# Attention in runs of four steps: four steps of logits, then their four products with v, instead of two and two

## Chip, cores, metric

One core of one Trainium2 chip. The metric is the device time of one execution in microseconds (us), median of several.

## The reference

A convolution block on x of shape (8, 512, 32, 32), fp32: group norm, a 1x1 convolution, then two bottlenecks, then a 1x1 convolution over everything and a residual. Each bottleneck is a 3x3 convolution, an attention over the 1024 positions with 4 heads of 64 channels, and a 1x1 convolution. What matters is the attention:

```python
q, k, v = (qkv[:, 0], qkv[:, 1], qkv[:, 2])
r = (rw + rh).reshape(1, HEADS, HD, hw)
logits = jnp.einsum('bhdi,bhdj->bhij', q, k + r) * HD ** (-0.5)
a = jax.nn.softmax(logits, axis=-1)
out = jnp.einsum('bhij,bhdj->bhdi', a, v)
```

8 images and 2 bottlenecks make 16 attention blocks. The kernel leaves the subtraction of the maximum out (and checks the sums at the end; a slower general path exists that is not taken here).

## The kernel before

A block has 4 groups: two pairs of heads (c) times two halves of 512 query positions. A group has 8 steps, each 128 key positions j. A step is: logits of both heads into one PSUM tile, exponential to SBUF (ScalarE), addition to acc for the softmax sums (VectorE), and the product with v, accumulated in PSUM. Steps go in pairs; a pair shares one pt tile. Each fp32 matmul here leaves two records in the trace (2048 records for the 1024 matmuls of the logits), so a step with its two heads has four records of logits and four of products. The code below is shortened; comments and `...` mark what was added and left out.

```python
def logits(pair):
    g, j0 = pair[0]
    c, half = groups[g]
    pt = act.tile([P, PAIR, 2, HALF], F32, tag="pt", name="pt", bufs=n_pt)     # n_pt = 3
    pts[pair[0]] = pt
    for i, (_, j) in enumerate(pair):
        ps = ps_big.tile([P, 2, HALF], F32, tag="big", name="l_ps")            # 3 buffers
        for hd in range(2):
            r = slice(hd * HD, (hd + 1) * HD)
            nc.tensor.matmul(ps[:, hd, :], kr[r, c, ts(j, P)], q[r, c, ts(half, HALF)],
                             start=True, stop=True)                            # L389
        nc.scalar.activation(pt[:, i], ps, AF.Exp, scale=SCALE)                # L393
    if j0 == 0:
        accs[g] = act.tile([P, 2, HALF], F32, tag="acc", name="acc", bufs=2)
        nc.vector.tensor_tensor(accs[g], pt[:, 0], pt[:, 1], ALU.add)          # L396
    else:
        for i in range(PAIR):
            nc.vector.tensor_tensor(accs[g], accs[g], pt[:, i], ALU.add)       # L399

def times_v(pair):
    ...
    for i, (_, j) in enumerate(pair):
        for hd in range(2):
            o = c * P + hd * HD
            nc.tensor.matmul(avs[g][hd * HD : (hd + 1) * HD, :], vT[:, j, o : o + HD],
                             pt[:, i, hd, :], start=(j == 0), stop=(j == NJ - 1))  # L410
    if j0 + PAIR == NJ:
        nc.scalar.copy(ao[:, c, ts(half, HALF)], avs.pop(g))

def divide(g):
    ...
    for hd in range(2):                                                        # L422
        nc.tensor.matmul(ps[hd * HD : (hd + 1) * HD, :], ones, acc[:, hd, :], start=True, stop=True)
    nc.vector.tensor_scalar(rs, ps, 1.0, None, ALU.mult, ALU.max, accum_out=smax[:, i : i + 1])
    nc.vector.tensor_reduce(smin[:, i : i + 1], rs, AX.X, ALU.min)
    nc.vector.reciprocal(rs, rs)                                               # L431
    nc.vector.tensor_tensor(dst, dst, rs, ALU.mult)                            # L433, dst in ao

for i in range(len(pairs) + 1):
    if i < len(pairs):
        logits(pairs[i])
    if i > 0:
        times_v(pairs[i - 1])
        g, j0 = pairs[i - 1][0]
        if j0 == 0 and g > 0:
            divide(g - 1)
divide(len(groups) - 1)
```

After the block comes the 1x1 convolution over ao (L555), first its half of the positions that does not need the last group, then the other half. As compiled, 12 of its 16 records stand ahead of the four that need the last group; these four are what the prediction calls the second half of L555.

## Time and profile before

| | before |
|---|---|
| time, median | 2860.6 us (2858.6 to 2861.4) |
| TensorE busy | 93% of the span |
| VectorE busy | 55% |
| ScalarE busy | 32% |
| a block, first logits to the first matmul on ao | 64.95 us, in 15 of 16 blocks |

The last line is taken from the starts of the matmuls in the trace. The lines of the page, the timeline and the waits are in the prediction.

### The profile page before, as it was taken

The page shows a single profiled execution, that of the slowest core. Times are in us where ns is not written, and L with a number is a line of the kernel's source. Part 1 is how long each engine was busy: PE and PEld are TensorE (multiplying, and loading weights), DVE is VectorE, ACT ScalarE, POOL GpSimd, SP SyncE. Part 2 cuts the span into 40 slices and gives each one's busy share as a digit, 9 for nine tenths or more (in the row PEclk, how much of TensorE's full clock was granted, in tenths as well). Part 3 has the DMA queues.
Part 4 walks back from the last instruction along what each step waited for, and adds up shares of the span by engine and source line. Part 5 has one row for each costly group of instructions (what it writes and reads, how often), then busy time and mean ns, then how long its engine had stood idle before and what let it go on. Part 6 is the DMA issues. An engine that isn't in the chain of part 4 may idle for free.

```text
span 2857.4 us, 24013 instructions
## 1 busy us (share of the span) xinstructions
PE 2670.4 (93%) x9506; PEld 1308.0 (46%) x9506; DVE 1582.2 (55%) x2116; ACT 923.6 (32%) x1209; POOL 72.0 (3%) x180
## 2 busy tenths in 40 slices
PE   2999999899998999989999899998999989999897
PEld 1626346263463534544354544545346363463633
DVE  5374734847347564575545665466644657437472
ACT  2242422424223332333324242242422424224241
POOL 2000000000000000000000000000000000000000
PEclk9999999999999999999999999999999999999998
DMA  9201011010110101101011000101012010110000
GB/s 356 87 1 67 1 59 67 1 67 2 57 67 1 67 15 44 67 16 51 30 42 55 34 34 30 63 34 61 6 44 81 1 67 1 52 67 1 0 1 31
DMA packets 25047, 130.23 MB, mean 46 GB/s; under 512 B 4448, under 2 KB 4960, under 8 KB 15200
## 3 DMA queue, kind: packets, MB, share of 16 engines
q1 hardware_dynamic: 14400, 97.00, 9.5%
q0 software_dynamic: 6784, 26.25, 2.4%
q10 hardware_dynamic: 3744, 5.37, 0.5%
q8 instruction: 77, 1.26, 0.2%
q14 instruction: 42, 0.34, 0.0%
HBM read 102.40 MB, written 26.21 MB: 45 GB/s over the span
## 4 chain that ended last, share of the span: by engine, by line
issue 56%; PE 37%; DVE 3%; POOL 1%; DMA 1%; ACT 0%; POOLq 0%; DVEq 0%; ACTq 0%; SPq 0%
PE ps L229 12%; PE l_ps L389 7%; PE av_ps L410 6%; PE c_mid L530 6%; PE c_end L530 3%; PE v_ps L360 2%; DVE acc L399 1%; DVE rs L431 1%; POOL out_dram L591 1%; PE s_ps L422 0%; DMA raw<-in_m_cv_w_dram 0%; DMA bnp<-in_cv_bn_dram 0%; DMA u<-u_new 0%; ACT pt L393 0%; POOL gr L320 0%
## 5 line engine op out<-in xcount | busy, mean ns | idle before, releaser
L393 ACT ACTIVATE pt<-l_ps 128x1024 f32<-128x1024 f32 x512 | 494.6, 1022 | 386.9 <-PE l_ps L389 386.9
L399 DVE TENSOR_TENSOR acc<-acc,pt 128x1024 f32<-128x1024 f32 x384 | 467.0, 1216 | 131.9 <-ACT pt L393 109.9
L389 PE MATMUL l_ps<-q,kr 64*128 64x512 f32 x2048 | 504.4, 613 | 0.0
L410 PE MATMUL av_ps<-pt,vT 128*64 128x512 f32 x2048 | 492.4, 604 | 0.0
L530 PE MATMUL c_mid<-v_in,u 128*128 128x256 f32 x1536 | 354.2, 388 | 70.7 <-DVE v_in L265 66.6
L530 PEld LDWEIGHTS c_mid<-v_in,u 128*128 128x128 f32 x1536 | 297.8, 195 | 127.1 <-issue 83.7
L389 PEld LDWEIGHTS l_ps<-q,kr 64*128 64x128 f32 x2048 | 177.6, 186 | 322.0 <-issue 314.5
L229 PE MATMUL ps<-xn,cv_sb 128*128 128x512 f32 x512 | 236.2, 624 | 48.1 <-DVE xn L325 48.1
L410 PEld LDWEIGHTS av_ps<-pt,vT 128*64 128x64 f32 x2048 | 125.6, 136 | 337.3 <-issue 264.2
L214 ACT ACTIVATE h<-ps,bh,sh 128x512 f32<-128x512 f32 x128 | 92.5, 773 | 521.5 <-PE ps L229 521.5
L229 PE MATMUL ps<-z,qkv_sb 128*128 128x512 f32 x512 | 229.2, 595 | 0.0
L229 PE MATMUL ps<-ypad,cv_sb 128*128 128x512 f32 x512 | 224.9, 592 | 0.0
L431 DVE RECIPROCAL rs<-rs 128x512 f32<-128x512 f32 x64 | 214.6, 3353 | 2.2
L530 PE MATMUL c_end<-v_in,u 128*128 128x256 f32 x768 | 181.9, 389 | 0.0
L229 PEld LDWEIGHTS ps<-xn,cv_sb 128*128 128x128 f32 x512 | 100.0, 198 | 178.3 <-issue 119.4
L530 PEld LDWEIGHTS c_end<-v_in,u 128*128 128x128 f32 x768 | 149.9, 195 | 22.6
L229 PEld LDWEIGHTS ps<-ypad,cv_sb 128*128 128x128 f32 x512 | 97.3, 190 | 122.5 <-issue 122.5
L279 DVE TENSOR_TENSOR sd<-c_mid,m 128x512 f32<-128x512 f32 x32 | 22.1, 691 | 228.3 <-ACT m L277 228.3
L229 PEld LDWEIGHTS ps<-z,qkv_sb 128*128 128x128 f32 x512 | 95.9, 190 | 106.5 <-issue 95.7
L396 DVE TENSOR_TENSOR acc<-pt 128x1024 f32<-128x1024 f32 x64 | 78.4, 1225 | 108.5 <-ACT pt L393 108.5
L585 DVE SCALAR_TENSOR_TENSOR t<-t,h 128x512 f32<-128x512 f32 x64 | 41.3, 687 | 171.2 <-ACT t L215 171.2
L277 ACT COPY m<-c_mid 128x512 f32<-128x512 f32 x32 | 18.7, 585 | 347.8 <-PE c_mid L530 347.8
(101 smaller groups left out, 2036.7 us busy)
## 6 DMA issues: line engine op xcount, KB each, us to landing
u<-u SPq DMA_DIRECT2D x64, 1152.0 KB, 6.9
x<-in_x_dram SPq DMA_DIRECT2D x32, 512.0 KB, 4.2
out_dram<-t POOLq DMA_DIRECT2D x64, 256.0 KB, 3.9
u<-u_new POOLq DMA_DIRECT2D x8, 1152.0 KB, 7.9
raw<-in_m_cv_w_dram SPq DMA_DIRECT2D x4, 1152.0 KB, 7.6
cv_sb<-in_cv_w_dram ACTq DMA_DIRECT2D x1, 2048.0 KB, 13.5
qkv_sb<-in_m_qkv_w_dram ACTq DMA_DIRECT2D x2, 768.0 KB, 12.9
cv_sb<-in_cv_w_dram ACTq DMA_DIRECT2D x1, 1024.0 KB, 9.1
```

The source lines that it names most:

```text
L214: nc.scalar.activation(h, ps, AF.Identity, scale=sh[:, k : k + 1], bias=bh[:, k : k + 1])
L229: nc.tensor.matmul(ps[:, half, :], w_of(k), rhs_of(k, half), start=(k == 0), stop=(k == nk - 1))
L360: nc.tensor.matmul(ps[:, j, :], z[:, k, ts(j0 + j, P)], qkv_sb[:, n, k, 2 * C : 3 * C], start=(k == 0), stop=(k == NM - 1),)
L389: nc.tensor.matmul(ps[:, hd, :], kr[r, c, ts(j, P)], q[r, c, ts(half, HALF)], start=True, stop=True,)
L393: nc.scalar.activation(pt[:, i], ps, AF.Exp, scale=SCALE)
L396: nc.vector.tensor_tensor(accs[g], pt[:, 0], pt[:, 1], ALU.add)
L399: nc.vector.tensor_tensor(accs[g], accs[g], pt[:, i], ALU.add)
L410: nc.tensor.matmul(avs[g][hd * HD : (hd + 1) * HD, :], vT[:, j, o : o + HD], pt[:, i, hd, :], start=(j == 0), stop=(j == NJ - 1),)
L431: nc.vector.reciprocal(rs, rs)
L530: nc.tensor.matmul(dst, us[k][:, pos, dx, :], vs[k][:, pos, :, dx : dx + F], start=(i == 0), stop=(i == NM * 3 - 1),)
L585: nc.vector.scalar_tensor_tensor(t, t, 1.0, h, ALU.add, ALU.mult)
L591: nc.gpsimd.dma_start(dst, t)
```

## The change

The intent is to alternate less often between logits and products. The change has a second side: before, the products of a pair stand one pair behind, after the logits of the next pair; now a run's products follow directly on its own logits. Nothing else is touched.

```diff
-            for i in range(len(pairs) + 1):
-                if i < len(pairs):
-                    logits(pairs[i])
-                if i > 0:
-                    times_v(pairs[i - 1])
-                    g, j0 = pairs[i - 1][0]
+            RUN = 2
+            for i in range(0, len(pairs), RUN):
+                for pair in pairs[i : i + RUN]:
+                    logits(pair)
+                for pair in pairs[i : i + RUN]:
+                    times_v(pair)
+                    g, j0 = pair[0]
                     if j0 == 0 and g > 0:
                         divide(g - 1)
             divide(len(groups) - 1)
```

## The prediction

> **What bounds the kernel now.** I read the page first, then the groups, then one attention block in the timeline, then the waits.
>
> ```profile
> PE 2670.4 (93%) x9506; PEld 1308.0 (46%) x9506; DVE 1582.2 (55%) x2116; ACT 923.6 (32%) x1209; POOL 72.0 (3%) x180
> ...
> L389 PE MATMUL l_ps<-q,kr 64*128 64x512 f32 x2048 | 504.4, 613 | 0.0
> L410 PE MATMUL av_ps<-pt,vT 128*64 128x512 f32 x2048 | 492.4, 604 | 0.0
> ```
>
> TensorE is busy 93% of the span, and the two attention groups (logits, L389; products with v, L410) show no idle time before them. So inside attention nothing but TensorE sets the pace, and a gain must come from TensorE itself. There are 16 attention blocks (8 images, 2 blocks each), each of 32 steps in 4 groups of 8. The profile's idle column cannot show the cost at stake, because a matmul's recorded time covers the pause ahead of the next one. The starts in the timeline can:
>
> ```profile
> 139.40 3.70 PE L389 MATMUL l_ps<-q,kr 64*128 64x512 f32 x16
> 143.03 1.94 PE L410 MATMUL av_ps<-pt,vT 128*64 128x512 f32 x8
> 144.90 0.70 PE L389 MATMUL l_ps<-q,kr 64*128 64x512 f32 x2
> ...
> 148.68 1.99 PE L389 MATMUL l_ps<-q,kr 64*128 64x512 f32 x8
> 150.60 1.94 PE L410 MATMUL av_ps<-pt,vT 128*64 128x512 f32 x8
> 152.47 0.70 PE L389 MATMUL l_ps<-q,kr 64*128 64x512 f32 x2
> ```
>
> Columns are start, extent, engine and group. A run of 8 logits records (two steps) lasts 150.60 - 148.68 = 1.92 us from start to next start; a run of 16, which the kernel before has once at the head of every block, lasts 143.03 - 139.40 = 3.63 us, not 3.84. So 8 more records cost 1.71 us, 0.428 us for each pair of records, and 0.21 us of each run of logits is fixed. For products, 8 records last 152.47 - 150.60 = 1.87 us; less 4 x 0.428 that leaves 0.15 us fixed. One round of logits and products is 152.47 - 148.68 = 3.79 us, with 0.353 us (unrounded starts) in its two changes of shape.
>
> **What bounds the end of a block.**
>
> ```profile
> 198.60 3.65 PE L410 MATMUL av_ps<-pt,vT 128*64 128x512 f32 x16
> 203.34 1.08 PE L422 MATMUL s_ps<-acc,ones 128*64 128x512 f32 x4 [1.09 <-DVE acc L399]
> 204.35 5.42 PE L555 MATMUL m_ps<-ao,m_sb 128*128 128x512 f32 x12
> 210.12 1.12 PE L555 MATMUL m_ps<-ao,m_sb 128*128 128x512 f32 x2 [0.36 <-DVE ao L433]
> ```
>
> There TensorE waits 1.09 us for VectorE's last addition to acc before it can form the last sums. The list of waits over the whole run (total, times, longest) says that this happens once in each block:
>
> ```profile
> PE s_ps L422 <- DVE acc L399: 17.7, 16, 1.4
> ```
>
> VectorE is late because, in each group, it has the division of the group before between its additions:
>
> ```profile
> 161.02 0.69 DVE L427 TENSOR_SCALAR_CACHE_REDUCE rs<-s_ps 128x512 f32<-128x512 f32 x1
> 161.63 0.08 DVE L427 DVE_READ_ACCUMULATOR rs<-s_ps 128x1 f32 x1
> 161.75 0.69 DVE L430 TENSOR_REDUCE smin<-rs 128x1 f32<-128x512 f32 x1
> 162.47 3.35 DVE L431 RECIPROCAL rs<-rs 128x512 f32<-128x512 f32 x1
> 165.74 1.16 DVE L399 TENSOR_TENSOR acc<-acc,pt 128x1024 f32<-128x1024 f32 x1
> 166.82 0.68 DVE L433 TENSOR_TENSOR ao<-ao,rs 128x512 f32<-128x512 f32 x1
> 167.42 3.88 DVE L399 TENSOR_TENSOR acc<-acc,pt 128x1024 f32<-128x1024 f32 x3
> ```
>
> From the start of rs to the end of the group's last addition is 171.30 - 161.02 = 10.28 us without a gap. That chain sets the end of a block, in both kernels.
>
> **What the Trainium skill says.** "TensorEngine Tiling (Array Packing)", section Tiling Modes, Key Properties: changing the tiling mode drains TensorE. Logits use 64 rows of the array (64*128 in the lines), products 64 columns (128*64), so each change of line is such a change, and the trace agrees: about 0.35 us per two changes. "TensorE: Matmul & The Clock Gate", Part 2, says that the engine pulls weight loads ahead of matmuls in flight. The trace agrees within a run, where the loads of L389 start a pair ahead (139.93 and 140.36 us, matmuls 0.43 us later), and shows it lost at a change, where the weight load sits idle 0.76 to 0.81 us and starts with its own matmul. "Trainium Kernel Development and Optimization", Reading a trace, warns that matmul busy time is a bad metric because matmuls are pipelined; here too, busy time is no measure of what is saved.
>
> **The change, part by part.** The compiled orders of VectorE, GpSimd and the load queue are the same instruction by instruction. On TensorE only the order of logits, products and the sums' matmuls moves; on ScalarE only the four copies of av_ps, which now stand ahead of the next group's exponentials. No instruction is added or removed.
>
> *Removed.* Before, a block runs 15 logits runs (the first double) and 15 product runs (the last double); after, 8 and 8. Seven rounds of two changes go: 7 x 0.353 = 2.47 us a block, 16 x 2.47 = 39.5 us in all, if nothing else sets the end.
>
> *Added waits inside a run of four steps.* PSUM holds three logits tiles, so step 4 waits for the exponential of step 1. In the existing run of 16 that starts at 140.57 and takes 1.02 us, so it is done 2.19 us into the run; the weight load of step 4 starts at 2.25 us, the normal 0.43 us after the one before. It fits by about 0.05 us: no wait. Step 4's exponential ends 4.94 us into the run (140.57 + 3.77), and its product comes at about 6.3 us. With the new copy of av_ps first at a group's head, the exponential still starts 1.18 us in (156.25, copy, 157.43), as elsewhere. The three pt buffers: each new pair needs the pair three back, already multiplied and added. No wait.
>
> *VectorE in the new order.* A round of four steps is 16 x 0.429 + 0.353 = 7.22 us; a group is two rounds and the sums' matmuls (0.86 us): 15.3 us, from 16.0 (172.25 - 156.25). VectorE has 8 steps in 7 additions and the division, from its first addition at 3.15 us after the group's start to the fourth step at about 7.0, when it takes rs (the sums are there at 6.5), and 10.28 us later, at 17.3 us, it is through: 2.0 us into the next group, whose first addition can only start at 3.15. So VectorE has about 1.1 us to spare per group: it does not set the pace, but it is filled to some 93%.
>
> *The end of a block.* The last group's products end 2 x 7.217 + 0.858 = 15.3 us after its start (the sums of the group before lie inside it), but acc is ready at 17.3. TensorE waits about 2.0 us for VectorE there, against 1.09 now. Measured from the start of the last group's first logits, acc is ready at 203.29 - 184.47 = 18.82 us before and 17.28 after: 1.54 us earlier. That start itself is 45.07 us into the block before and 6 x 7.217 + 2 x 0.858 = 45.02 after: 0.05 us. Sum: 1.59 us a block, 25.4 us over 16. What follows a block (second half of L555, activation, next convolution) hangs on it in series and moves with it. 2860.8 - 25.4 = 2835.4 us, 0.9% less.
>
> **The rivals.**
> 1. *VectorE does not set the end:* the full 39.5 us, 2821 us. For it: VectorE is busy only 55% in the page. Against it: the 1.09 us wait is already there in all 16 blocks.
> 2. *The fourth step waits for PSUM.* The margin is 0.05 us; if exponentials came 0.15 us late in each of 16 x 7 new runs, that takes back up to 17 us of TensorE time; part of this is hidden in the wait at the end: 2840 to 2850 us. Against it: 16 runs in this trace show the same tight fit with no stall.
> 3. *VectorE becomes the bound of every group,* for instance when its first addition comes later than 3.15 us or additions slow: then groups stretch towards 16 us and the gain dwindles: 2850 us or above. Against it: 1.1 us to spare.
> 4. *Products lose their lead over the exponentials,* since no logits stand between step 4 and its product: margin 1.3 us, so I give this little.
>
> **Range and chances.** The centre is the VectorE-bound sum. Down, towards rival 1, it can go as far as 2821 but hardly further; up, rivals 2 and 3 together. So 2824 to 2845. Over 2% faster would need 57 us, more than all removed changes are worth; over 2% slower needs 3.6 us more per block, for which no wait is in sight. Hence 0.02, 0.96, 0.02.
>
> **What would show it.** Right: in the timeline runs of 16 logits of 3.63 us and 16 products of about 3.58 us, 8 each per block; no idle before L389 and L410; the wait of s_ps for acc grown from 1.1 to about 2.0 us in 16 places; a block from first logits to its last sums' matmul of 62.3 us instead of 63.9. Wrong: idle before l_ps put down to pt (rival 2), idle of VectorE gone between groups (rival 3), idle before av_ps (rival 4), or an unchanged 1.1 us wait with 2821 us (rival 1). My sum fails if the cost of a change of shape is not the same in the longer runs of products, which the trace before shows only once a block.

## The result, and the profile after

The changed kernel takes 2836.6 us median (2831.5 to 2837.2, 4 runs). The ratio of the fast runs is 0.9913, 95% interval 0.9896 to 0.9930; it is the mean time of one kernel's fast runs over that of the other's of the same rounds, so not quite the ratio of the medians. The interval lies clear of 1: 24 us less. 25.4 had been predicted.

The first block in the timeline of TensorE (start, extent, engine, group):

```profile
139.67 3.70 PE L389 MATMUL l_ps<-q,kr 64*128 64x512 f32 x16
143.30 3.65 PE L410 MATMUL av_ps<-pt,vT 128*64 128x512 f32 x16
146.88 3.70 PE L389 MATMUL l_ps<-q,kr 64*128 64x512 f32 x16
150.52 3.65 PE L410 MATMUL av_ps<-pt,vT 128*64 128x512 f32 x16
```

Runs of 16 records, as forecast: logits 143.30 - 139.67 = 3.63 us, products 146.88 - 143.30 = 3.58 us, a round 7.21 us where two rounds took 7.57. No line shows idle time: the fourth step of logits does not wait for its PSUM tile, nor a product for its exponential.

The end of that block, in the timeline of TensorE:

```profile
196.40 3.65 PE L410 MATMUL av_ps<-pt,vT 128*64 128x512 f32 x16
201.97 1.08 PE L422 MATMUL s_ps<-acc,ones 128*64 128x512 f32 x4 [1.91 <-DVE acc L399]
202.97 5.42 PE L556 MATMUL m_ps<-ao,m_sb 128*128 128x512 f32 x12
```

and the list of waits over the whole run (total, times, longest):

```profile
PE s_ps L422 <- DVE acc L399: 30.9, 16, 2.3
```

The products are done 2.46 us earlier in the block than before (start of the sums less the wait, 60.39 us against 62.85 after the first logits), but the wait for acc has grown from 1.09 to 1.91 us: a third of the saving goes into a longer wait. From first logits to the last sums' matmul it is 201.97 - 139.67 = 62.30 us, from 63.94. The last group on VectorE, in its timeline:

```profile
187.84 1.23 DVE L396 TENSOR_TENSOR acc<-pt 128x1024 f32<-128x1024 f32 x1 [1.23 <-ACT pt L393]
...
191.64 0.68 DVE L427 TENSOR_SCALAR_CACHE_REDUCE rs<-s_ps 128x512 f32<-128x512 f32 x1
...
198.03 3.88 DVE L399 TENSOR_TENSOR acc<-acc,pt 128x1024 f32<-128x1024 f32 x3
```

VectorE sits idle for 1.23 us at the head of the third and of the fourth group of a block (1.1 had been worked out; the first two, which have no division before them, leave it idle longer) and works without a marked wait from 187.84 to 201.91, when acc is ready: 17.2 us after the group's first logits at 184.69 (17.28 forecast).

Over 16 blocks, first logits to the first matmul on ao, the sums are 1039.5 us before and 1013.3 after: 26.2 us, 1.64 a block.

**What varies outside the blocks.** The stages between the two blocks of one image contain stretches in which TensorE has little to do, and the clock granted to it falls. They differ from image to image and run to run. Four of the 16 such stretches, in windows of the trace, first of the kernel before, then of the kernel after (columns: window and length, busy time and count of PE, PEld (TensorE's loading of weights), DVE, ACT and POOL, mean granted clock, DMA share, GB/s):

```profile
204.35:274.77 70.42, 61.73 (x226) 43.71 (x224) 34.89 (x61) 12.73 (x20) 0.00 (x0) 0.93 0.18 67
```

```profile
202.97:272.79 69.82, 61.13 (x227) 43.14 (x225) 34.93 (x61) 12.73 (x20) 0.00 (x0) 0.95 0.19 68
891.20:962.11 70.91, 62.58 (x226) 43.98 (x225) 34.93 (x61) 12.73 (x20) 0.00 (x0) 0.93 0.18 67
1236.89:1306.80 69.91, 61.21 (x227) 43.32 (x225) 34.92 (x61) 12.73 (x20) 0.00 (x0) 0.95 0.19 68
```

The same work takes 69.8 to 70.9 us. The mean clock alone does not sort all 16 (in the kernel after one stretch of 70.47 us has 0.95, one of 70.30 us has 0.93); shorter windows show more. In the first stretch of the kernel before the granted clock is 0.50 from 214.9 to 224.9 us, in the first of the kernel after only from 215.5 to 222.1, and 1.00 on both sides; in the stretch of 70.91 us it is 0.50 a second time, from 891.3 to 894.6, right after the wait for acc at the end of a block, as in no other block of this run. The Trainium skill, "TensorE: Matmul & The Clock Gate", Part 1, says that the clock gate's window is free-running and that its cost varies from run to run; the trace agrees as far as such stretches in one execution differ by 1.1 us. Of the four runs of the kernel after, the one of 2831.5 us, which is the profiled one, had a mean granted clock of 0.984, the three of 2836.4 to 2837.2 had 0.980 or 0.981. This is why I compare blocks, and why times of whole executions agree with sums over blocks only to some 6 us.

### The profile page after: what moved, and what is told of

Its sections match the earlier page's. It is cut to its first block, busy times and chain, and to the rows that moved or that the text cites. A ratio compares the mean times of both kernels' runs of the same rounds, so it can differ in the third digit from the quotient of the medians.

```text
span 2829.9 us, 23965 instructions
## 1 busy us (share of the span) xinstructions
PE 2622.3 (93%) x9506; PEld 1323.9 (47%) x9506; DVE 1579.6 (56%) x2116; ACT 912.3 (32%) x1209; POOL 73.1 (3%) x180
## 4 chain that ended last, share of the span: by engine, by line
issue 56%; PE 35%; DVE 4%; POOL 1%; DMA 1%; ACT 1%; POOLq 0%; DVEq 0%; ACTq 0%; SPq 0%
PE ps L229 11%; PE l_ps L389 6%; PE av_ps L410 6%; PE c_mid L531 6%; PE c_end L531 3%; PE v_ps L360 2%; DVE acc L399 1%; DVE rs L431 1%; POOL out_dram L592 1%; ACT pt L393 1%; PE s_ps L422 0%; DVE xn L325 0%; DMA raw<-in_m_cv_w_dram 0%; DMA bnp<-in_cv_bn_dram 0%; DVE acc L396 0%
## 5 line engine op out<-in xcount | busy, mean ns | idle before, releaser
L393 ACT ACTIVATE pt<-l_ps 128x1024 f32<-128x1024 f32 x512 | 483.1, 1030 | 285.3 <-PE l_ps L389 285.3
L410 PE MATMUL av_ps<-pt,vT 128*64 128x512 f32 x2048 | 475.8, 598 | 0.0
L389 PE MATMUL l_ps<-q,kr 64*128 64x512 f32 x2048 | 474.1, 602 | 0.0
L389 PEld LDWEIGHTS l_ps<-q,kr 64*128 64x128 f32 x2048 | 187.2, 186 | 284.0 <-issue 222.7
L410 PEld LDWEIGHTS av_ps<-pt,vT 128*64 128x64 f32 x2048 | 135.6, 136 | 316.4 <-issue 261.5
L229 PE MATMUL ps<-xn,cv_sb 128*128 128x512 f32 x512 | 230.0, 609 | 54.8 <-DVE xn L325 54.8
L229 PE MATMUL ps<-ypad,cv_sb 128*128 128x512 f32 x512 | 224.9, 592 | 0.0
L351 DVE TENSOR_TENSOR kr<-ps,rw_sb 128x512 f32<-128x512 f32 x64 | 41.2, 686 | 160.4 <-PE ps L229 160.4
```

What stands on the lines that cost most here:

```text
L229: nc.tensor.matmul(ps[:, half, :], w_of(k), rhs_of(k, half), start=(k == 0), stop=(k == nk - 1))
L351: nc.vector.tensor_tensor(dst, img(ps[:, half, :]), rw, ALU.add)
```

## The experiments

My theory: seven rounds of two changes of shape, 0.353 us each round, go from TensorE's work in each block (2.47 us), and about 0.9 us of that is taken back at the end of the block, where VectorE's additions and the division of the group before set the time. Rivals: TensorE sets the end of a block and changes cost less than 0.353 us; or the fixed cost of a run belongs not to the shape but to waits at a run's start.

### Taking the reciprocal out of both orders

```diff
-                nc.vector.reciprocal(rs, rs)
+                nc.vector.tensor_scalar(rs, rs, 0.0, 1e-8, ALU.mult, ALU.add)
```

The result is wrong (relative error 0.17).

> Order of before, reciprocal (3.35 us) replaced by a constant written with a tensor_scalar (results wrong on purpose). Theory (VectorE sets the end of a block): last sums no longer wait for acc (1.1 us) nor the second half of L555 for ao (0.36 us): 16 x 1.45 = 23 us less, about 2837 us. Rival (TensorE alone sets the end of a block and the changes of shape cost less than 0.353 us): about 2860, unchanged.

> Order of after with the same constant. Theory: with VectorE off the path all of the removed changes show, 16 x 2.47 = 39.5 us between this run and the same edit of before: about 2798 us. Rival: the difference stays what it is between before and after, 24 us, so about 2813 if the edit alone gains 23, or 2836.

Measured: 2832.0 us in the order of before (ratio 0.9904, 0.9889 to 0.9919), 2806.0 in the order of after (0.9812, 0.9798 to 0.9825). The constant took 0.43 us instead of 3.35. The edit alone gained 28 us in the old order (23 expected), but the orders differ by 26 us, not by 39.5. The number failed, and I would have had to give the theory up had the trace not shown why. In blocks the difference is 63.64 - 61.61 = 2.03 us, 32.5 us in all; the rest between the blocks was 5.7 us longer in the second profile, which fits the varying clock above (mean granted clock 0.983 and 0.979). Of the missing 0.44 us a block, the end of a block of the second kernel, timelines of TensorE and then VectorE, shows where it is:

```profile
196.33 3.65 PE L410 MATMUL av_ps<-pt,vT 128*64 128x512 f32 x16
200.19 1.08 PE L422 MATMUL s_ps<-acc,ones 128*64 128x512 f32 x4 [0.21 <-DVE acc L399]
```

```profile
194.92 5.21 DVE L399 TENSOR_TENSOR acc<-acc,pt 128x1024 f32<-128x1024 f32 x4 [0.75 <-ACT pt L393]
```

VectorE is still the last: its four additions start when the first exponential of the run arrives (it had been waiting 0.75 us) and end at 200.13, while without a wait the sums' matmul would have come at 199.81: 3.48 us after the start of the last 16 products, as in the same edit of the old order (202.68 - 199.20). So 0.38 us were lost there again. A cheap division does not take VectorE off the end of this order: the exponentials of four steps come together, and so do their additions. The edit was not the clean test that I had meant it to be.

### The same addition taken from VectorE in both orders

Only the last step of a block is summed by TensorE, in the time in which it would wait (the diff is shortened: the choice of parts is written in fewer lines, and last_pt starts as an empty list):

```diff
                     for i in range(PAIR):
+                        if g == len(groups) - 1 and j0 + i == NJ - 1:
+                            last_pt.append(pt[:, i])
+                            continue
                         nc.vector.tensor_tensor(accs[g], accs[g], pt[:, i], ALU.add)
 ...
+                parts = [last_pt[0], acc] if g == len(groups) - 1 else [acc]
+                for part in parts:
                     for hd in range(2):
                         nc.tensor.matmul(
-                            ps[hd * HD : (hd + 1) * HD, :], ones, acc[:, hd, :], start=True, stop=True
+                            ps[hd * HD : (hd + 1) * HD, :], ones, part[:, hd, :],
+                            start=(part is parts[0]), stop=(part is parts[-1]),
                         )
```

> Order of after; in the last group of each block the addition of the eighth step to acc leaves VectorE (1.33 us) and TensorE sums that step itself, two more matmuls with ones (0.86 us) while it would wait. The result stays right. Theory (VectorE's additions set the end of a block): acc is ready 1.33 us earlier, the two new matmuls lie in the 1.9 us wait, the wait before the matmuls on acc shrinks to nearly nothing and a block ends about 1.2 us earlier: 19 us less, about 2817 us. Rival (TensorE sets the end): 16 x 0.86 = 14 us more, about 2850 us.

> Order of before, with the last step of a block summed by TensorE as in the run of that name; the result is right. Together with that run this is the change alone, with VectorE's last addition off the path in both. Theory: a block is then TensorE's in both orders, and the two differ by the full 7 x 0.353 = 2.47 us a block, 39.5 us: 2809.8 + 39.5 = about 2849 us, and 64.5 us a block against 62.04. Rival (seven rounds cost less than that): the difference stays near 24 us, about 2834.

Measured, results right: 2809.8 us in the order of after (ratio 0.9824, 0.9811 to 0.9838), 2852.3 in the order of before (0.9972, 0.9960 to 0.9985). The end of a block in the timeline of TensorE, order of after:

```profile
199.81 1.03 PE L429 MATMUL s_ps<-pt,ones 128*64 128x512 f32 x4
200.67 1.03 PE L429 MATMUL s_ps<-acc,ones 128*64 128x512 f32 x4
201.63 5.42 PE L564 MATMUL m_ps<-ao,m_sb 128*128 128x512 f32 x12
```

The same in the order of before:

```profile
202.51 1.03 PE L429 MATMUL s_ps<-pt,ones 128*64 128x512 f32 x4
203.37 1.03 PE L429 MATMUL s_ps<-acc,ones 128*64 128x512 f32 x4
204.33 5.42 PE L563 MATMUL m_ps<-ao,m_sb 128*128 128x512 f32 x12
```

No wait for acc is left, in either order. With the first logits at 139.59 and 139.83 us, the two orders now differ by 64.50 - 62.04 = 2.46 us a block: the 2.47 of the prediction. Over 16 blocks that is 39 us (the times differ by 42). So the change removes 39 us of TensorE time, and the kernel as changed lets 24 to 26 of it through, because VectorE sets the end of each block. The gain of this edit in the order of after is 63.31 - 62.04 = 1.27 us in most blocks, 20 us in the sums over blocks; the time fell by 27, more than the 19 expected, and the 7 between them are of the size of the variation outside the blocks. Against the control of the same rounds further down (2833.1 us, the blocks of the kernel after) it fell by 23.

### What a change of shape costs

Two small matmuls of 128 columns in the middle of each run of logits, ahead of the real ones, which overwrite them. In one kernel they have the logits' shape, in the other the products' (both edits in one listing, shortened):

```diff
                     ps = ps_big.tile([P, 2, HALF], F32, tag="big", name="l_ps")
+                    if dummy and i == 0:          # the second pair of a run
+                        for hd in range(2):
+                            # logits' shape:
+                            nc.tensor.matmul(ps[:, hd, 0:128], kr[r, c, ts(j, P)], q[r, c, 0:128], start=True, stop=True)
+                            # or products' shape:
+                            nc.tensor.matmul(ps[hd * HD : (hd + 1) * HD, hd, 0:128], ones, q[:, c, 0:128], start=True, stop=True)
```

> Order of after, with two small matmuls (128 columns) of the shape of the logits in the middle of each run of four steps; their result is overwritten, so the output is right. Theory: no change of shape, so only their own time, 0.2 to 0.4 us each run; on the path in 6 of a block's 8 runs (the last group's lie in the wait for acc): 96 x 0.3 = 29 us, about 2865 us. In the timeline the run of logits is 0.2 to 0.4 us longer.

> The same with the two small matmuls in the shape of the products. Theory (a change of shape costs): 0.353 us more for each run than with the small matmuls of the logits' shape, 96 x 0.353 = 34 us more than that run, near 2900 us. Rival (the pause belongs to the waits or the change of operands at the start of a run, not to the shape): the two runs with small matmuls agree within 0.5%.

Measured: 2858.4 us and 2887.8 us, both right; 29.4 us apart (34 expected), 2.18 us a block in the trace, 34.9 us in all. Both times lie below the 2865 and 2900 expected, since the small matmuls took 0.22 us a run and not 0.3. A block has eight such runs, but what the last two add is largely taken out of the wait for acc at the end (30.9 us over 16 blocks in the kernel after, 23.7 in the first of these, 14.2 in the second), so about six of them count. One run in the timeline, first with small matmuls of the logits' shape, then of the products':

```profile
138.87 1.99 PE L395 MATMUL l_ps<-q,kr 64*128 64x512 f32 x8
140.69 0.39 PE L390 MATMUL l_ps<-q,kr 64*128 64x128 f32 x4
140.91 1.89 PE L395 MATMUL l_ps<-q,kr 64*128 64x512 f32 x8
142.72 3.65 PE L416 MATMUL av_ps<-pt,vT 128*64 128x512 f32 x16
```

```profile
139.91 1.99 PE L394 MATMUL l_ps<-q,kr 64*128 64x512 f32 x8
141.83 0.44 PE L389 MATMUL l_ps<-q,ones 128*64 128x128 f32 x4
142.20 1.99 PE L394 MATMUL l_ps<-q,kr 64*128 64x512 f32 x8
144.11 3.65 PE L415 MATMUL av_ps<-pt,vT 128*64 128x512 f32 x16
```

The first run of logits takes 142.72 - 138.87 = 3.85 us, 0.22 more than the 3.63 of the kernel after: the small matmuls' own time. The second takes 144.11 - 139.91 = 4.20, another 0.35 us for two changes of shape. The second kind also brings a new operand (ones), and a run's first matmul has waits to pass; but the sums' matmuls, which have other operands than the products around them, a wait for VectorE and the same shape, stand between products in the kernel after at 0.86 us for their four records (160.36 - 159.50), the bare price of four records. So the cost goes with the shape, and the rival falls.

### Runs of eight

A longer run needs four pt tiles. To make room for the fourth, w_tmp of the convolution goes into the pt buffers and h of the activation into those of rs:

```diff
-            h = act.tile([P, HALF], F32, tag="h", name="h", bufs=2)
+            h = act.tile([P, HALF], F32, tag="rs", name="h", bufs=2)
-            tmp = act.tile([P, 3, NT, 2, F], F32, tag="wt", name="w_tmp", bufs=1)
+            tmp = act.tile([P, 3, NT, 2, F], F32, tag="pt" if n_pt == 4 else "wt", name="w_tmp", bufs=n_pt if n_pt == 4 else 1)
-    s = stages(act, small, ps_big, ps_av, 3)
+    s = stages(act, small, ps_big, ps_av, 4)
```

(u_tmp, once at the start, also has bufs=4.) The control has this alone; the next has RUN = 4 as well; the last has RUN = 4 and the last step of a block on TensorE.

> Control for the next run: order of after with a fourth pt tile, for which two small work tiles of the convolution share other tiles' buffers. Theory: nothing waits for pt or these tiles, so within 0.2% of after, 2831 to 2842 us, and 63.3 us a block. Rival (the third pt tile holds the exponentials back): faster by 5 us or more.

> Eight steps of logits, then their eight products (runs of four pairs), with the room of the control. Four more rounds of changes of shape go: 4 x 0.353 = 1.41 us a block of TensorE time. Theory: in the new order VectorE adds all eight steps of the last group ahead of the division of the group before, so acc no longer holds up the last sums, but the division before (5.5 us) holds up theirs; worked through, the second half of L555 starts 1.6 us earlier: 25 us less, about 2811 us. Rival (the end of a block is TensorE's, so the cost of changes is all that counts): 16 x (1.41 + 1.91) = 53 us less; rival (eight steps outrun the exponentials and stall on PSUM): no gain, idle time before l_ps.

> Both: runs of eight steps, and the last step of a block summed by TensorE. Theory: VectorE has 1.33 us less ahead of its two last divisions, so 1.3 us a block less than with runs of eight alone: about 2790 us. Rival: no gain over runs of eight, since acc is ready in time there anyway.

Measured, all right: control 2833.1 us and 63.31 us a block, exactly that of the kernel after, so room alone does nothing. Runs of eight 2804.8 us (ratio 0.9807, 0.9792 to 0.9822). With both 2791.6 us (0.9762, 0.9747 to 0.9777), the fastest of all, 2.4% under the kernel before. The end of a block with runs of eight, in TensorE's timeline:

```profile
198.76 1.03 PE L422 MATMUL s_ps<-acc,ones 128*64 128x512 f32 x4
199.72 1.12 PE L556 MATMUL m_ps<-ao,m_sb 128*128 128x512 f32 x2
201.77 4.56 PE L556 MATMUL m_ps<-ao,m_sb 128*128 128x512 f32 x10 [0.92 <-DVE ao L433]
207.28 1.98 PE L556 MATMUL m_ps<-ao,m_sb 128*128 128x512 f32 x4 [0.96 <-DVE ao L433]
```

The wait for acc is gone, but the two divisions now come one after the other on VectorE, and the matmuls on ao wait for each. The last four of them start 207.28 - 139.95 = 67.33 us after the first logits; in the kernel after they start at 208.75, 69.08 us after. That is 1.75 us in this block. The second block of an image gains more (there the kernel after needs 69.42 us, runs of eight 67.34), so that over 16 blocks it is 31.8 us against the kernel after, with 32 us in the times, and 30.0 us against the control, with 28 in the times; 25 were forecast. So four more rounds, worth 1.41 us of TensorE time, and a better order on VectorE are both in it. The rival that eight steps outrun the exponentials fails: no idle time before l_ps. With the last step on TensorE as well, another 13 us go (21 expected for 1.3 us a block): the last four on ao start 66.41 us after the first logits, 0.93 us earlier in this block and 0.81 on the mean of 16, not 1.3, because VectorE now waits 0.31 us for the sums, which the two added matmuls delay. TensorE and VectorE end such a block almost together.

### Runs of one pair

```diff
-            RUN = 2
+            RUN = 1
```

> Two steps of logits and at once their own two products (runs of one pair): 16 rounds a block instead of 8, and no other logits between an exponential and its product. Theory: 8 x 0.353 = 2.8 us more a block than after for the changes of shape, and about 0.3 us of waiting in each of the 16 rounds, since a product comes 1.92 us after its logits began and the exponential is ready at 2.2: 5 us. Some 7 us a block, 2836 + 118 = about 2954 us, with waits of av_ps for pt. Rival (only changes of shape count): 2836 + 45 = 2881 us, no such waits.

Measured: 3185.1 us (ratio 1.1133, 1.1116 to 1.1150), right, and far beyond what either theory said. The timeline of TensorE shows an order that I had not looked for:

```profile
142.65 1.12 PE L389 MATMUL l_ps<-q,kr 64*128 64x512 f32 x2
143.70 1.08 PE L410 MATMUL av_ps<-pt,vT 128*64 128x512 f32 x4
144.71 1.98 PE L389 MATMUL l_ps<-q,kr 64*128 64x512 f32 x6
147.00 1.08 PE L410 MATMUL av_ps<-pt,vT 128*64 128x512 f32 x4 [0.32 <-ACT pt L393]
```

The scheduler pulled one head's logits of the next pair in between the two products, since the second product has to wait. So a block has 55 changes of shape in place of the 15 after and 29 before (counted in the traces), and one head's logits stand alone. In the run of six records that follows, the records of the head that is left over start 0.429 us apart (145.669 and 146.098 us), so two records of one head alone take 0.86 us, as long as all four records of a step with both heads, whose matmuls begin 7 ns apart in the trace. A round (from 144.71 us to the next run of six records at 150.07) lasts 5.36 us in place of the 3.785 of before, and 1.53 of the 1.58 are told: 0.86 us because one step's two heads run apart (twice 0.86 us instead of once), 0.35 for two more changes, 0.32 waiting for the exponential. The wait that I had expected is there (rival 4 of the prediction is real at this run length); the rest came from an order that is a matter of the scheduler. As a measure of the cost of one change this run is spoilt.

## Why the prediction was right

**Removed rounds: right.** 7 x 0.353 = 2.47 us a block; with VectorE out of the way in both orders 2.46 were measured, and the small matmuls give 0.35 us for two changes on their own.

**No new waits inside a run: right.** No idle time before logits or products in the trace after. The prediction gave the fourth step 0.05 us of margin for PSUM, and it held: all 128 runs of logits in the profiled execution last 3.63 us to the next start.

**VectorE fills up but does not set the pace of a group: right.** Idle 1.23 us at the head of the last two groups, 1.1 forecast.

**The end of a block takes part of the gain back: right.** Wait for acc 1.91 us, "about 2.0" forecast; 62.30 us to the last sums' matmul, 62.3 forecast. A block gained 1.64 us, 1.59 forecast. Moving one addition away from VectorE returned 1.27 us a block, which it could not have done had TensorE set the end.

**The sum: right,** 2835.4 forecast, 2836.6 measured; but the agreement to 1 us is partly luck, since stages outside the blocks vary by several us (the profiled run took 2831.5), and the prediction started from 2860.8 where the median before is 2860.6. The 26.2 us of the sums over blocks against 25.4 is the fairer test.

**What I had wrong later:** the test with the cheap reciprocal. There I took it that VectorE would be off the path, and did not add up that four additions follow the exponentials of the last run, whatever the division costs. And for runs of one pair I took the order of the source for the order that runs.

## What to carry to other kernels

When two kinds of matmul alternate on an engine that is never idle, compare run lengths in the timeline: a run of 16 that takes less than two runs of 8 gives the fixed cost of a change, even though no wait shows it. Then ask what ends the stage in which the runs lie; here a third of the removed time went into a wait for VectorE at the end of each block, and giving the waiting TensorE one addition of VectorE's brought it back with more. Check the compiled order before reading a short-run experiment as a measure of one cost.

## What the Trainium skill lacked or had wrong

- "TensorEngine Tiling (Array Packing)", Tiling Modes, Key Properties, says that changing the mode drains TensorE but gives no cost: here 0.35 us for two changes, between 64-row logits and 64-column products in fp32 with 512 columns.
- The same page gives a gain of up to 2x for two tiles as theory; "TensorE: Matmul & The Clock Gate", Part 3, has measured gains for three tiles and more, but none for two: here two heads' logits take 0.86 us together and one head's alone 0.86 us as well, so the pair runs at twice the rate.
- No page that I read gives the time of a reciprocal on VectorE: 3.35 us for 128x512 fp32, against 0.43 us for a tensor_scalar and 0.69 us for a tensor_tensor of the same size. "VectorE: DVE Perf Modes" names the iterative divide without a duration.
